# Attention rows: where denominators and numerators stand on the tensor engine, and which PSUM banks they use

## The chip, the core and the metric

The kernel runs on one core of one Trainium2 chip. The core's engines work side by side and each takes its own instructions strictly in order: the tensor engine (PE) multiplies matrices into PSUM, the vector engine (DVE) and the scalar engine (ACT) read PSUM and SBUF and write back, GpSimd (POOL) does little here, and the sync engine (SP) issues most of the DMAs. An instruction starts when its engine has come to it and the semaphores it waits for are set. PSUM has eight banks of 128 partitions by 512 float32 values. The metric is the device time of one execution in microseconds (us); lower is better.

## The reference

Two blocks of gated cross-attention and feed-forward work on `x` (8 batches of 512 tokens, 512 wide). The change lies in the first attention, which is linear attention with 16 heads of 32:

```
q    = feature_map(layernorm(x) @ Wq.T)          # x+1 if x>0 else exp(x)
gate = sigmoid(layernorm(x) @ Wg.T + bg)
k, v = split(ctx @ Wkv.T);  k = feature_map(k)
kv_summary = einsum('bhsd,bhse->bhde', k, v);  k_sum = k.sum(axis=-2)
z    = 1.0 / (einsum('bhld,bhd->bhl', q, k_sum)[..., None] + EPS)
attn = einsum('bhld,bhde->bhle', q, kv_summary) * z
x    = x + tanh(g_xattn[0]) * (attn * gate) @ Wo.T
```

The denominators are the einsum under `z`, the numerators the one with `kv_summary`. Everything after it (a feed-forward block, a softmax attention, an expert block) is untouched. All arithmetic is float32.

## The kernel before

**Rows.** The attention stage is a loop over the eight batches; the text calls a batch a row, 0 to 7. Each of the three large products of a row (Q, G for the gate, and O for the output) is done in seven block products instead of eight, in the order 1, 2, 6, 5, 7, 4, 3. One block product is four matmuls of 128x128 by 128x256 in the program, eight records in the profile, since each float32 matmul makes two passes. Products 1, 6, 7, 4 accumulate in a bank called x, 5 and 3 in w, and 2 in z, so that the rows of the profile say `x_q`, `w_g`, `z_xa_down` and so on (`xa_down` is O).

**Order by hand.** `steps` gives the first five products of a unit and keeps 4 and 3 back until the next unit's first product is done. In row b the program therefore lists Q1, O4, O3 (of row b-1's output), Q2, Q6, Q5, Q7; then G1, Q4, Q3, G2, G6, G5, G7; then O1 (the output of row b-1), G4, G3, O2, O6, O5, O7. The output of a row is one row late, because its attention needs the row's denominators spread out over the partitions.

**Order by a scheduler.** In this stage `in_order` holds neither the tensor nor the vector nor the scalar engine. What the program lists for these three is put in its final order, engine by engine, by a scheduler when the kernel is built; at run time the order is fixed. While `"tensor"` is in `in_order`, PE keeps the listed order: that is done around the numerators.

**The parts that the steps speak of.**

- `features` (L613 to L621): two ACT activations, relu and exp (L619, L620), then one DVE operation that writes a part of `q` (L621). After Q3 the last part takes a DVE addition (`qs_q`, L1157), the two activations and L621.
- `denominators` (L1187): four 32-column matmuls of `q` with `ksum` into one bank `pd`; DVE adds epsilon into `z` (L1195); two reciprocals of 128x256 (L1198); `z` goes to DRAM (`over`), and `spread` reads it back broadcast over the partitions. It is a generator, and each `next` lists one more of these pieces. Before, its first piece (matmuls and L1195) is listed at O1.
- `gated` (L1212) multiplies the gate's `th` by what `spread` brought, in the next row's Q.
- `numerators` (L1219): sixteen 32x32 matmuls of `q` with `summary` into four banks `pn0` to `pn3`.
- `attended` (L1232): DVE multiplies each `pn` by `th` into `a` (L1243, four operations of 128x512), and forms the sums s1, s2 and a difference (`combine_inner`, L895 to L897). O1 reads `a`.
- `GUp` (L1164): the gate. It writes `th`, a tile that has **one buffer** (pool `attention_units`, `bufs=1`), with additions on DVE (L1178) and tanh on ACT (L1183); the additions free the banks z, w of G.
- `normed` (L471): the norm of row b+1, with four ACT operations `xn_xa` and four transposes `pt_xa` on PE into PSUM, copied by ACT (L517).

**PSUM.** Pool `ps` has four banks, shared in turn by `pt_xa`, `pd` and `pn`. Pool `acc` has four, used in turn by the x, w and z banks of Q, G and O. `numerators` takes all four `ps` banks at once.

**Listing before.** In row b, the numerators of row b-1 and `attended` are listed between Q7 and G1; the denominators of row b at O1:

```
        if done:
            attended(done[0], done[2], numerators(*done[0:2]))
        g = GUp(b)
        den = denominators(b, q.q)
```

Row 0 has no earlier row: all of its denominators' pieces are listed after G7. Row 7 has nothing after it: the pieces of its denominators are listed from G6 on, and its numerators follow G7 in the same row.

Of the kernel before, what the change touches and what calls it, by code (L numbers as in the profile page):

```python
# [21 lines left out]
F32 = mybir.dt.float32  # L22
# [6 lines left out]
PSUM = bass.MemoryType.PSUM  # L29

P = 128
B, S, D = 8, 512, 512
# [11 lines left out]
H2 = 256  # L44
# [24 lines left out]
def flamingo_kernel(  # L69
# [40 lines left out]
    phase = ExitStack()  # L110
# [5 lines left out]
    bank = {"ps": ps}  # L116

    def psum(name):
        return bank["ps"].tile([P, 512], F32, tag="ps", name=name)

    idle_banks = []

    def acc_bank(name):

        if not idle_banks:
            return bank["acc"].tile([P, 2, H2], F32, tag="acc", name=name), None
        assert len(idle_banks) > 0
        n = idle_banks.pop(0)
        return bank["acc"].tile([P, 2, H2], F32, tag=f"acc{n}", name=name, bufs=1), n

    def temp(name):
        return work.tile([P, 512], F32, tag="t2", name=name, bufs=8)

    def halves(t):

        return t.rearrange("p (n t) -> p n t", t=H2)
# [25 lines left out]
    def load_x(ph, b):  # L162
        if ph == "xa0" and b % 4 == 3:
            t = awork.tile([P, NT, D], F32, tag="x4", name=f"x_{ph}{b}")
        else:
            t = work.tile([P, NT, D], F32, tag="x", name=f"x_{ph}{b}", bufs=3)
        if ph == "xa0":
            src = x[ts(b, S), :].rearrange("(t p) d -> p t d", p=P)
        else:
            src = between[ph, b]  # L170

        queue = nc.scalar if ph == "xa0" and b > 1 else nc.sync
        with here("scalar"):
            queue.dma_start(out=t, in_=src)
        xs[ph, b] = t
# [3 lines left out]
    def flush():  # L179
        while stores:  # L180
            store_x(*stores.pop(0))
# [468 lines left out]
    def cross_attention(b):  # L650
# [63 lines left out]
        yield  # L714

        lent, n = acc_bank(f"pr_{b}_3")
        idle_banks.append(n)
        pr = [psum(f"pr_{b}_{t}") for t in range(3)] + [lent.rearrange("p n t -> p (n t)")]
# [91 lines left out]
    OPENS, CLOSES = (1, 5, 2), (4, 3, 2)  # L810

    class Unit:
# [5 lines left out]
        def step(self, m):  # L818
            name = BANK[m]
            if m in OPENS:  # L820
                self.banks[name], self.numbers[name] = acc_bank(f"{name}_{self.tag}")
            self.product(m, self.banks[name])
            self.after(m, self.banks[name])
            if m in CLOSES and self.numbers[name] is not None:
                idle_banks.append(self.numbers[name])

        def weights(self, m):
# [64 lines left out]
    def combine_inner(at, prefix=""):  # L892

        a11, a12, a21, a22, s1, s2 = (inner[prefix + k][:, at, :] for k in INNER)
        nc.vector.tensor_tensor(s1, a21, a22, ALU.add)  # L895
        nc.vector.tensor_tensor(s2, s1, a11, ALU.subtract)
        nc.vector.tensor_tensor(a21, a11, a21, ALU.subtract)  # L897
# [97 lines left out]
    class SplitDown(Unit):  # L995
# [6 lines left out]
        OPENS, CLOSES = (2, 4, 1, 5), (2, 4, 7, 3)  # L1002
# [70 lines left out]
        def gated(self, dst, src):  # L1073
            nc.vector.scalar_tensor_tensor(dst, src, GATE[self.ph], dst, ALU.mult, ALU.add)
# [111 lines left out]

    def denominators(b, q):  # L1187

        pd = psum(f"pd_{b}")
        for c in range(NC):  # L1190
            nc.tensor.matmul(pd[ts(c, HD), :], lhsT=kv[b][1][:, c, :], rhs=q[:, c, :], start=True, stop=True)
            in_order.add("tensor")
        in_order.discard("tensor")
        z = temp(f"z_{b}")
        nc.vector.tensor_scalar(z, pd, ATT_EPS, None, ALU.add)  # L1195
        yield
        for r in range(2):
            nc.vector.reciprocal(z[:, ts(r, H2)], z[:, ts(r, H2)])  # L1198
            yield
        over[b] = dram.tile([P, S], F32, tag=f"over{b}", name=f"over_{b}")  # L1200
        nc.sync.dma_start(out=over[b], in_=z)
        yield
# [16 lines left out]
    def numerators(b, q):  # L1219

        summary = kv[b][0]
        pn = [psum(f"pn{h}_{b}") for h in range(NC)]
        in_order.add("tensor")
        for c in range(NC):
            for h in range(NC):
                rows = ts(h, HD)
                nc.tensor.matmul(
                    pn[h][ts(c, HD), :], lhsT=summary[rows, c, :], rhs=q[rows, c, :], start=True, stop=True
                )
        return pn  # L1230

    def attended(b, th, pn, ahead=lambda b, th, half: None):  # L1232

        if b < B - 1:
            a = aunits.tile([P, 2, 2, 2, H2], F32, tag="a", name=f"a_{b}")
        else:
            a = work.tile([P, NC, S], F32, tag="xnT", name=f"a_{b}").rearrange(
                "p (r c) (n t) -> p r c n t", c=2, n=2
            )
        for h in range(NC):  # L1240
            if h % 2 == 0:
                ahead(b, th, h // 2)
            nc.vector.tensor_tensor(  # L1243
                a[:, :, h // 2, h % 2, :], halves(th[:, h, :]), halves(pn[h]), ALU.mult
            )
        for k in ("s1", "s2"):
            inner["x" + k] = aunits.tile([P, 2, H2], F32, tag=k, name=f"{k}_xa0_{b}")
        for r in range(2):
            for c in range(2):
                inner[f"xa{r + 1}{c + 1}"] = a[:, r, c]  # L1250
        combine_inner(slice(0, 2), "x")
# [12 lines left out]
    def steps(units, late=late):  # L1264

        for u in units:
            for n, m in enumerate(u.order[: u.head]):
                yield u, m
                if n == 0:
                    yield from late  # L1270
                    late.clear()
            late.extend((u, k) for k in u.order[u.head :])
# [9 lines left out]
    def some(prep):  # L1282
        if prep not in ready and next(prep, None) == "last":
            ready.add(prep)
# [50 lines left out]
        pass  # L1335
    set_aside()
    first.close()
    bank["acc"] = phase.enter_context(tc.tile_pool(name="acc", bufs=4, space=PSUM, reuse_waits="tile"))
    aunits = phase.enter_context(tc.tile_pool(name="attention_units", bufs=1, reuse_waits="tile"))
    in_order -= {"tensor", "vector", "scalar"}  # L1340
    builder = build_first()
    done = None
    ticks = iter(range(10**6))

    def tick():

        if next(ticks) % 2:
            next(builder, None)

    for b in range(B):  # L1350
        prep = work_list[b + 1][2]
        if b == B // 2 + 1:
            nc.vector.tensor_scalar(b2_sb, b2_sb, gate_ff0, None, ALU.mult)
        q = QUp(b)
        for n, (u, m) in enumerate(steps([q])):
            u.step(m)
            if done and n in (1, 3):
                gated(done[0], done[2], n // 2)
            if b == B - 1 and n == 1:
                load_x("ff0", 0)  # L1360
            if n == 4:
                flush()
                if b < B - 1:
                    some(prep)
            tick()
        if done:
            attended(done[0], done[2], numerators(*done[0:2]))
        g = GUp(b)
        den = denominators(b, q.q)
        for n, (u, m) in enumerate(steps([g])):  # L1370
            u.step(m)
            in_order.discard("tensor")
            tick()
            if n == 1:
                if b + 2 < B:
                    load_x("xa0", b + 2)
                elif b + 1 == B:
                    load_x("ff0", 1)
            if b == B - 1 and n > 3:
                next(den, None)  # L1380
            if n == 3 or n > 3 and not done:
                some(prep)
        if not done:
            for _ in den:
                pass
            spread(b)
        if b == B - 1:
            for _ in den:
                pass
            spread(b)  # L1390
            pn = numerators(b, q.q)
        for n, (u, m) in enumerate(steps([ODown(done[0])] if done else [])):
            u.step(m)
            in_order.discard("tensor")
            if b < B - 1:
                next(den, None)
                if n == 6:
                    spread(b)
            elif n == 6:
                attended(b, g.th, pn, gated)  # L1400
            if n in ((0, 1, 3, 5) if b < B - 1 else (6,)):
                some(prep)
            tick()
        for _ in prep:
            pass
        done = b, q.q, g.th
# [52 lines left out]
    for u, m in [*steps([ODown(B - 1)]), *late]:  # L1459
# [6 lines left out]
        ps=stack(tc.tile_pool(name="ff_ps", bufs=3, space=PSUM, reuse_waits="tile")),  # L1466
        acc=stack(tc.tile_pool(name="ff_acc", bufs=1, space=PSUM, reuse_waits="tile")),
    )
    idle_banks += range(5)
    bank["ringb"] = stack(tc.tile_pool(name="ringb", bufs=1, reuse_waits="tile"))  # L1470
    for _ in range(MORE):
        next(loads)
# [125 lines left out]
```

## Time and profile before

| | us |
|---|---|
| median of three runs | 2057.13 (2056.67 to 2058.53) |
| the profiled execution, its own time | 2056.86 |
| its span in the profile | 2055.1 |
| PE busy | 2040.4 |
| DVE busy | 1501.5 |
| ACT busy | 629.3 |
| attention stage of rows 1 to 7, first numerators to the first feed-forward product | 81.25 to 378.07 |

The page says that a busy PE is not PE at its peak. A matmul is pipelined: one pass of 128x256 is recorded with some 0.38 us, but eight of them that follow each other start every 1.73 us together. The views that the prediction uses are the timelines of the engines (start, duration, engine, line, operation, tiles, count, and in brackets the idle time before with the instruction that ended it), the table by stretches of time, and the list of waits.

The critical chain on the page is of the end of the execution and does not reach back to the attention stage, so the stage has to be read from the timelines.

### The profile page before, as it was taken

How to read it: one execution, taken by the hardware profiler on the slowest of the kernel's cores; microseconds unless marked ns; L12 is line 12 of the kernel's file. 1: busy time of each engine (PE TensorE's matmuls, PEld its weight loads, DVE VectorE, ACT ScalarE, POOL GpSimd, SP SyncE). 2: the span in 40 equal slices, each digit the busy share in tenths (PEclk: the TensorE clock that was granted, in tenths of full speed). 3: DMA queues.
4: the chain of work that ended last, by engine and by line, in shares of the span. 5: the costliest groups of instructions: out<-in, count | busy, mean ns of one | idle time of the engine just before them, and what ended most of it. 6: DMA issues, size and time to landing. Idle time of an engine off the chain costs nothing. (4 is left out here: it accounts for less than half of the span.)

```text
span 2055.1 us, 35088 instructions
## 1 busy us (share of the span) xinstructions
PE 2040.4 (99%) x12796; PEld 1814.5 (88%) x12796; DVE 1501.5 (73%) x2989; ACT 629.3 (31%) x1294; POOL 97.7 (5%) x124
## 2 busy tenths in 40 slices
PE   9999999999999999999999999999999999999998
PEld 5888887898989999999989898898989898898988
DVE  4787888575758677676859676877777776777758
ACT  4533443323242423233242322213122222212121
POOL 3000000000000000000001010100000010100000
PEclk9999999999999999999999999999999999999999
DMA  6376546698888887888868768585867768585865
GB/s 203 132 220 193 180 140 192 237 299 278 300 280 280 280 295 249 293 278 282 294 218 284 228 195 281 172 283 178 281 201 242 231 197 279 174 282 155 275 204 170
DMA packets 304235, 484.67 MB, mean 236 GB/s; under 512 B 37056, under 2 KB 103776, under 8 KB 299968
## 3 DMA queue, kind: packets, MB, share of 16 engines
q1 hardware_dynamic: 296624, 455.65, 69.6%
q10 hardware_dynamic: 5856, 23.20, 3.1%
q0 software_dynamic: 1584, 3.57, 0.7%
q8 instruction: 103, 1.69, 0.3%
q14 instruction: 68, 0.56, 0.1%
HBM read 413.04 MB, written 69.27 MB: 235 GB/s over the span
## 5 line engine op out<-in xcount | busy, mean ns | idle before, releaser
L856 PE MATMUL x_ff<-S_ff,w_ff 128*128 128x256 f32 x1280 | 304.2, 380 | 0.0
L856 PE MATMUL w_ff<-S_ff,w_ff 128*128 128x256 f32 x1280 | 303.4, 380 | 0.0
L856 PE MATMUL x_ff<-xnT_ff,w_ff 128*128 128x256 f32 x1280 | 294.5, 379 | 0.0
L868 ACT COPY u_ff<-x_ff 128x512 f32<-128x512 f32 x240 | 139.9, 584 | 475.4 <-PE x_ff L856 447.6
L856 PEld LDWEIGHTS x_ff<-S_ff,w_ff 128*128 128x128 f32 x1280 | 240.5, 190 | 40.2 <-issue 6.5
L856 PEld LDWEIGHTS w_ff<-S_ff,w_ff 128*128 128x128 f32 x1280 | 239.0, 190 | 32.2 <-issue 1.4
L856 PEld LDWEIGHTS x_ff<-xnT_ff,w_ff 128*128 128x128 f32 x1280 | 237.8, 190 | 30.8 <-ACT a_ff L916 0.4
L1051 PE MATMUL x_ff_down<-w_ff_down,split_ff_down 128*128 128x128 f32 x1344 | 157.9, 275 | 0.0
L1051 PEld LDWEIGHTS x_ff_down<-w_ff_down,split_ff_down 128*128 128x128 f32 x1344 | 153.9, 192 | 0.0
L856 PE MATMUL z_ff<-xnT_ff,w_ff 128*128 128x256 f32 x640 | 151.4, 379 | 0.0
L1065 DVE TENSOR_TENSOR part_ff_down<-part_ff_down 128x128 f32<-128x128 f32 x315 | 85.3, 288 | 67.5 <-ACT part_ff_down L1078 60.1
L856 PEld LDWEIGHTS z_ff<-xnT_ff,w_ff 128*128 128x128 f32 x640 | 119.8, 190 | 15.3
L1051 PE MATMUL w_ff_down<-w_ff_down,split_ff_down 128*128 128x128 f32 x896 | 105.3, 275 | 0.0
L1051 PEld LDWEIGHTS w_ff_down<-w_ff_down,split_ff_down 128*128 128x128 f32 x896 | 102.6, 192 | 0.0
L911 DVE TENSOR_TENSOR a_ff<-w_ff,u_ff 128x512 f32<-128x512 f32 x64 | 43.9, 686 | 72.8 <-ACT u_ff L868 72.7
L916 ACT ACTIVATE a_ff<-a_ff,b_sb 128x256 f32<-128x256 f32 x128 | 58.1, 501 | 94.1 <-DVE a_ff L911 94.1
L939 DVE SCALAR_TENSOR_TENSOR g_ff<-th_ff,x_ff 128x512 f32<-128x512 f32 x48 | 32.8, 684 | 70.3 <-ACT th_ff L938 70.3
L1051 PE MATMUL w_ff_down<-w_ff_down,s_ff 128*128 128x128 f32 x672 | 81.5, 275 | 0.0
L1051 PE MATMUL x_ff_down<-w_ff_down,a_ff 128*128 128x128 f32 x672 | 80.4, 275 | 0.0
L1051 PEld LDWEIGHTS w_ff_down<-w_ff_down,s_ff 128*128 128x128 f32 x672 | 79.4, 192 | 0.8
L1051 PEld LDWEIGHTS x_ff_down<-w_ff_down,a_ff 128*128 128x128 f32 x672 | 78.4, 192 | 0.5
L949 DVE TENSOR_TENSOR up_ff<-w_ff,u_ff 128x512 f32<-128x512 f32 x96 | 65.6, 684 | 17.7 <-ACT u_ff L868 17.7
(258 smaller groups left out, 3328.3 us busy)
## 6 DMA issues: line engine op xcount, KB each, us to landing
w_ff_down<-stream_ff SPq DMA_DIRECT2D x680, 256.0 KB
w_ff<-ff_up SPq DMA_DIRECT2D x560, 256.0 KB
stream_ff<-build_ff_down SPq DMA_DIRECT2D x49, 448.0 KB
x_ff<-x_ff SPq DMA_DIRECT2D x16, 1024.0 KB
share<-shares SPq DMA_DIRECT2D x64, 256.0 KB
ff_up<-build_ff_up SPq DMA_DIRECT2D x42, 256.0 KB
x_ff<-x_xa ACTq DMA_DIRECT2D x8, 1024.0 KB
x_ff<-x_ff ACTq DMA_DIRECT2D x8, 1024.0 KB
```

The costliest lines, as they stand in the source:

```text
L856: nc.tensor.matmul(p[:, n, :], lhsT=w[:, c, ts(n, P)], rhs=moving, **self.mark(m, 2 * n + c),)
L868: nc.scalar.copy(self.s[m], p)
L911: nc.vector.tensor_tensor(h, p, s, ALU.add)
L916: nc.scalar.activation(h[:, n, :], p[:, n, :], AF.Gelu, bias=b1_sb[:, f : f + 1])
L939: nc.vector.scalar_tensor_tensor(g, th, 1.0, p, ALU.add, ALU.mult)
L949: nc.vector.tensor_tensor(u, p, s, ALU.add)
L1051: nc.tensor.matmul(p[bank][:, place, :], lhsT=operand[k][:, c, :], rhs=w[at // 4][:, ts(at % 4, P)], start=bank not in opened, stop=True, ...
L1065: return lambda: nc.vector.tensor_tensor(m(k), m(k), m(by), ALU.add)
```

## The change

Three things are edited.

1. **The place.** The numerators of row b-1 with `attended` are no longer listed before G1. They are listed at step 5 of G, after G5, and directly ahead of them `next(den, None)` lists the denominators' matmuls and the addition that makes `z`. The next pieces move up by one step: in rows 1 to 6 the two reciprocals and the DMA are listed at O1, G4 and G3 (before: at G4, G3 and O2). In row 7 they are listed from G7 on, and in row 0 after G7.
2. **The bank.** `pd` no longer comes from pool `ps`. It takes a bank out of the list `idle_banks` and puts it straight back at the end of the list, so it is lent by the accumulators.
3. **The accumulators' banks.** Pool `acc` has four named banks with one buffer each. `acc_bank` takes the one that has been idle longest, and a unit gives its bank back when its last product on it is done. The fall-back to a rotating pool is gone.

```diff
     def acc_bank(name):
-        if not idle_banks:
-            return bank["acc"].tile([P, 2, H2], F32, tag="acc", name=name), None
-        assert len(idle_banks) > 0
         n = idle_banks.pop(0)
         return bank["acc"].tile([P, 2, H2], F32, tag=f"acc{n}", name=name, bufs=1), n
...
-            if m in CLOSES and self.numbers[name] is not None:
+            if m in CLOSES:
                 idle_banks.append(self.numbers[name])
...
     def denominators(b, q):
-        pd = psum(f"pd_{b}")
+        pd, n = acc_bank(f"pd_{b}")
+        idle_banks.append(n)
+        pd = pd.rearrange("p n t -> p (n t)")
...
-    bank["acc"] = phase.enter_context(tc.tile_pool(name="acc", bufs=4, space=PSUM, reuse_waits="tile"))
+    bank["acc"] = phase.enter_context(tc.tile_pool(name="acc", bufs=1, space=PSUM, reuse_waits="tile"))
+    idle_banks += range(4)
...
-        if done:
-            attended(done[0], done[2], numerators(*done[0:2]))
         g = GUp(b)
         den = denominators(b, q.q)
         for n, (u, m) in enumerate(steps([g])):
             u.step(m)
             in_order.discard("tensor")
+            if n == 5:
+                next(den, None)
+                if done:
+                    attended(done[0], done[2], numerators(*done[0:2]))
             tick()
...
-            if b == B - 1 and n > 3:
+            if b == B - 1 and n > 5:
                 next(den, None)
...
-    idle_banks += range(5)
+    idle_banks[:] = range(5)
```

## The prediction, made before the changed kernel had run

> **What bounds the kernel now.** First the page's busy shares: PE is busy for almost the whole span and at full granted clock throughout, so a microsecond of PE idleness in any stage is a microsecond of time.
>
> ```profile
> PE 2040.4 (99%) x12796; PEld 1814.5 (88%) x12796; DVE 1501.5 (73%) x2989; ACT 629.3 (31%) x1294; POOL 97.7 (5%) x124
> PEclk9999999999999999999999999999999999999999
> ```
>
> Then the table by stretches, cut at the first numerator record of rows 1 to 7 (stretch; length, busy time and count by engine):
>
> ```profile
> 81.25:121.67 40.42, 40.42 (x225) 33.70 (x224) 33.04 (x56) 17.04 (x31) 1.21 (x2) 1.00 0.56 165
> 121.67:163.72 42.05, 40.97 (x225) 33.55 (x225) 32.56 (x53) 17.13 (x31) 4.39 (x2) 1.00 0.81 243
> 163.72:204.98 41.26, 40.96 (x225) 33.54 (x224) 36.43 (x57) 16.89 (x31) 2.18 (x2) 1.00 0.57 174
> 204.98:245.41 40.43, 40.43 (x225) 33.71 (x224) 32.48 (x54) 17.43 (x31) 1.70 (x2) 1.00 0.53 174
> 285.84:326.94 41.10, 40.70 (x225) 33.63 (x224) 33.49 (x54) 17.42 (x31) 1.58 (x2) 1.00 0.55 180
> ```
>
> A clean row lasts 40.42; three rows are longer, by 1.63, 0.84 and 0.68: 3.1 us of stalls in rows 2, 3 and 6. The list of PE's waits between 60 and 380 us agrees: `x_g` behind ACT's `u_g` copy, `x_xa_down` behind DVE, and in row 7 `pd` twice behind L621 (0.7 and 0.4). So the stage has little to win: 3.1 us of stalls, about 2 us in row 7, and changes of tile size on PE. It has much to lose, because PE has no slack and DVE is 80% busy.
>
> What the change can save on PE stands in the timeline of row 5 (start, duration):
>
> ```profile
> 203.16 1.89 PE L856 MATMUL x_q<-S_xa,w_q 128*128 128x256 f32 x8
> 204.98 1.14 PE L60 MATMUL pn<-q,summary 32*32 32x512 f32 x32
> 206.05 1.99 PE L60 MATMUL x_g<-xnT_xa,w_g 128*128 128x256 f32 x8
> 207.88 1.89 PE L856 MATMUL x_q<-xnT_xa,w_q 128*128 128x256 f32 x8
> 209.61 1.89 PE L856 MATMUL w_q<-S_xa,w_q 128*128 128x256 f32 x8
> ```
>
> Read the differences of starts: a product takes 1.73 (207.88 to 209.61), 1.82 when `pn` follows and 1.83 behind it. Numerators cost 1.07 plus 0.09 and 0.10 for changing the tile size. The denominators in the same way: 1.82 before them, 1.00 (220.06 to 221.06), 0.05 behind.
>
> **Part 1: the two follow each other.** The Trainium skill, "TensorEngine Tiling (Array Packing)", Key Properties, says that changing the tiling mode drains the engine and changing only the tile does not. By that rule 128x32 after 32x32 is still a change, so four changes a row become three, not two. By the row: 0.09+0.05+0.09+0.10 = 0.33 becomes 0.09+0.05+0.10 = 0.24. Saved: 0.1 us a row; by a reading in which "follow each other" means one mode, 0.15. I take 0.1 in each of rows 1 to 6: **-0.6** (row 7 below).
>
> **Part 2: DVE's order.** In the built program of the changed kernel DVE's order in every row 1 to 7 is: last `q` (L621), `z` (L1195), both reciprocals, and only then the four products `a`, then `th` from `z_g`. Before, the `a` ran 9 to 12 us ahead of `z` (209.04 to 212.91 in row 5). Now they queue behind it:
>
> ```profile
> 221.20 0.69 DVE L1195 TENSOR_SCALAR z<-pd 128x512 f32<-128x512 f32 x1 [0.27 <-PE pd L60]
> 221.92 3.37 DVE L1198 RECIPROCAL z<-z 128x256 f32<-128x256 f32 x2
> ```
>
> `z` starts 0.14 after PE has gone on from `pd` (221.06); the reciprocals end at 225.29. Call E the moment PE leaves `pd`: reciprocals end at E+4.2, the first `a` (0.68) at E+4.9, the next three 0.60 apart (E+5.5, 6.1, 6.7).
>
> On PE, after E: `pn` 1.07, G7 with its change of size 1.83, so at E+2.9 it comes to the first transpose `pt_xa` of the next row's norm. Its PSUM bank is the one of `pn0` (four `ps` banks, all four taken by `pn`), and in the built program it waits for the first `a`. It is at the head of PE's queue; G4, O1 and all else stand behind it. Stall: 4.9-2.9 = **2.0 us a row**, rows 1 to 6: **+12.0**. In before this transpose stood about 16 us behind `pn`.
>
> Here a rule decides. "VectorE: DVE Perf Modes", Walkthrough, Mode 1x, in the Trainium skill gives one result a cycle; with 0.96 GHz ("Trainium Kernel Development and Optimization", NeuronCore Architecture) a 256-wide reciprocal would be an estimated 0.27 us, the first `a` would be done at E+2.1, and there would be no stall. The row says 1.69 each (3.37 for two), six times that; the same page remarks that a reciprocal is an iterative divide with a repeat count of 8, by which it would be an estimated 2.1 each and the stall 2.9. I take the row.
>
> **Part 3: q comes late for pd.** `pd` moves from 5 products after Q3's end (G2, G6, G5, G7, O1) to 3. Let T be the start of G2 (211.34 in row 5); `pd` is due at T+5.27. Its third matmul needs the last L621. ACT's built order in rows 1 to 5 is relu, the copy `u_g` of G6, exp; the copy waits for G6:
>
> ```profile
> 214.99 0.59 ACT L868 COPY u_g<-x_g 128x512 f32<-128x512 f32 x1
> 215.47 0.63 ACT L620 ACTIVATE fe_q<-fe_q 128x512 f32<-128x512 f32 x1
> ```
>
> exp ends at 216.10 = T+4.76, L621 (0.68, no longer behind the `a`) at T+5.5, `pd` goes on at 5.55: 0.3 late. If the two halves of `pd` do not overlap, it is up to 1.0 (row 7 of before shows two halves of 0.98 each). Below nothing is excluded: PE is at the instruction already. I take 0.3, five rows: **+1.5** (0 to 5). In row 6 exp is ahead of the copy: 0.
>
> **Part 4: th has one buffer.** `th` of row b may be written only when the `a` of row b-1 have read it, so G's additions stand behind the four `a`: `z_g` is freed at E+7.3 (a's end 6.7, plus 0.6). By disuse, O1 gets just that bank and waits for it. PE, after the stall: transpose 0.5, G4 1.73, so at O1 at E+7.15: +0.15 in rows 1, 2, 4, 5, 6. In row 3 a 128x896 operation of the weight building (1.08, L60) stands between: +1.1. G3 then waits for the `th` of `w_g` (E+9.1) about when PE gets there: 0.3 in all. The other transposes wait for ACT's `xn_xa`, which stand behind `th`'s tanh: I find them at about E+10.8 when PE needs them at E+10.85; nothing, but without margin. Sum **+2.2** (0 to 4). `pd`'s own lent bank was `w_q`'s, long read: nothing.
>
> **Part 5: what goes.** The 3.1 us in rows 2, 3 and 6 came of L621, `qs_q` and `u_g` behind the `a`, sums and building work on DVE. With the `a` moved behind `pd`, the q chain has DVE to itself: **-3.1** (0 if other work takes the place).
>
> **Part 6: rows 0 and 7, the tail.** Row 7: both numerators stand on either side of G7. The second set needs all four banks of the first, so it finishes about 1.0 behind the last `a`: E+7.7 = T+14.0 with E = T+6.3 (exp is early here). Before, from T (333.30) to its end (344.97) it was 11.67, without the first set (1.17). So 14.0-1.2-11.7 = **+1.1**, in which the two stalls of `pd` that go (1.1) and its halves (1.0) are already counted. Row 0: `pd` is cut by a transpose after its first matmul, which costs one more half, 1.0, and fills 0.4 that PE filled with other work anyway: **+0.6**. Tail to 378: `z` of row 7 is ready 3.7 earlier against T, so the 0.57 stall at 369.35 (DVE) may go: **-0.5**.
>
> SP's queue has the same DMAs in the same order; `over` is issued earlier after its row's `pd` and nothing is moved past it. POOL is as before in this stage. From the first feed-forward product on, the orders of PE, DVE and ACT are the same in both kernels, and the list of waits has 0.8 us for PE there in all, so nothing gives the loss back.
>
> **Sum.** -0.6+12.0+1.5+2.2-3.1+1.1+0.6-0.5 = +13.2 us. On the profiled execution's own time of 2056.86 (1.8 around its span of 2055.1) that is 2070.1; on the median 2057.13 it is 2070.3. I say **2070**.
>
> **Rivals.**
>
> *A. The stall is there and nothing else is won* (the old stalls stay in other places, `pd` in two halves): parts 3 at 5 and 5 at 0 give 13.2+3.5+3.1 = +19.8, 2077. For it: DVE's load a row is the same 33 us, only moved. Against: the q chain is what stalled PE, and it is now ahead of everything.
>
> *B. Faster: the stall is not there.* One mechanism: the first `a` is done before PE reaches the transpose, at E+2.9. Place: DVE between `z` and `a`. It needs the two reciprocals to last 1.4 together or less instead of 3.37. Then part 2, part 4 and about 2 us of row 7's wait fall away (12.0+2.2+2.0): 13.2-16.2 = -3.0, 2054. Against: 16 reciprocals of before, median 1.74.
>
> *C. The stall is hidden*: other waits of PE in the rows already hold the same time, so that only the change in rows 0 and 7 shows: 2057 to 2060. Against: four of the six rows had none.
>
> *D. The change doesn't do what it says:* excluded by the built order for rows 1 to 7 (`pd`, then `pn`, with nothing between); it fails only in row 0, where there is nothing above.
>
> **Numbers.** The forecast's own case 0.82, A 0.12, C 0.04, B 0.02. Range: low, parts 3 and 4 at nothing and rows 0 and 7 at half: 13.2-4.5=+8.7, 2065.5, less a little for a shorter stall, 2064; high, to most of A, 2076. Under 0.2% (4.1 us), about what a measurement of this kernel can't tell from no change: slower 0.95, same 0.04, faster 0.01.
>
> **What would show it.** In the profile after, the first `pt_xa` of each of rows 1 to 6 with about 2.0 us of idle PE before it, released by DVE `a` L1243; reciprocals directly ahead of the `a`; rows of about 42.8 between numerators; the waits for `u_g` and `qs_q` gone; `pd` with about 0.3 of idle or two halves; `pn` of row 7 waiting 2 us and more for `a`. Wrong: rows of 40 us, or the `a` ahead of the reciprocals in time, or idle PE of another kind that outweighs this one.

## The result, and the profile after

| | before | after |
|---|---|---|
| median (lowest to highest), six runs each | 2057.63 (2056.67 to 2059.22) | 2073.49 (2072.39 to 2074.59) |
| profiled execution, its own time / span | 2056.86 / 2055.1 | 2072.94 / 2071.2 |
| first feed-forward product starts at | 378.07 | 394.16 |
| from there to the end of the span | 1677.0 | 1677.0 |

The ratio is 1.0077, 95% interval [1.0067, 1.0087]: slower by 15.9 us; 2070 was forecast, 2064 to 2076 the range. All of it (394.16-378.07 = 16.09) arises in the attention stage, none comes back later. Line numbers after are one to three lower than before (L1194 is `z`, L1197 the reciprocals, L1242 `a`, L511 the transposes, L618 the last part of `q`).

The busy row of the page, and the table by stretches cut at the first numerator of rows 1 to 7 (stretch; length; busy time and count of PE, weight loads, DVE, ACT, POOL; granted clock; DMA):

```profile
PE 2045.7 (99%) x12796; PEld 1816.0 (88%) x12796; DVE 1503.1 (73%) x2989; ACT 629.8 (30%) x1294; POOL 97.0 (5%) x124
```

```profile
93.69:137.48 43.79, 41.85 (x226) 33.67 (x224) 33.74 (x53) 17.00 (x31) 2.59 (x2) 1.00 0.61 173
137.48:180.45 42.97, 41.07 (x226) 33.67 (x224) 32.94 (x54) 17.22 (x31) 1.71 (x2) 1.00 0.58 175
180.45:223.14 42.69, 40.86 (x226) 33.75 (x224) 33.88 (x53) 17.34 (x31) 1.70 (x2) 1.00 0.66 196
223.14:266.12 42.98, 41.09 (x227) 33.68 (x225) 32.42 (x52) 17.23 (x31) 1.58 (x2) 1.00 0.52 164
308.80:352.38 43.58, 41.15 (x228) 33.48 (x224) 38.40 (x64) 17.82 (x32) 1.59 (x2) 1.00 0.56 167
```

A row lasts 42.7 to 43.8 where it lasted 40.4 to 42.1, and the second column (PE busy) has grown far less than the length: PE stands still for the rest. PE's list of waits between 55 and 400 us names the reason (who waits, for whom; sum, times, longest):

```profile
PE pt_xa L511 <- DVE a L1242: 10.9, 6, 1.8
PE pn L60 <- DVE a L1242: 1.7, 1, 1.7
PE x_q L853 <- ACT u_q L865: 0.6, 1, 0.6
PE x_xa_down L969 <- DVE x_xa L985: 0.5, 1, 0.5
```

One row of it, row 4, in the timelines of PE and of DVE (start, duration, instruction, idle time before with its releaser):

```profile
223.14 1.14 PE L60 MATMUL pn<-q,summary 32*32 32x512 f32 x32
224.21 1.99 PE L60 MATMUL x_g<-S_xa,w_g 128*128 128x256 f32 x8
228.04 0.63 PE L511 MATMUL pt_xa<-ident,xn_xa 128*128 128x128 f32 x4 [1.83 <-DVE a L1242]
230.46 1.99 PE L969 MATMUL x_xa_down<-w_o,a 128*128 128x256 f32 x8
232.29 1.97 PE L853 MATMUL w_g<-S_xa,w_g 128*128 128x256 f32 x8
```

```profile
223.26 0.69 DVE L1194 TENSOR_SCALAR z<-pd 128x512 f32<-128x512 f32 x1 [1.15 <-PE pd L60]
223.99 3.37 DVE L1197 RECIPROCAL z<-z 128x256 f32<-128x256 f32 x2
227.27 2.41 DVE L1242 TENSOR_TENSOR a<-th,pn 128x512 f32<-128x512 f32 x4
```

PE leaves `pd` at 223.14 (the moment that the prediction calls E) and could go on from `pn` and G7 at 226.04 (224.21 and 1.83 behind). It then waits until 228.04, E+4.90, for the first `a`, which DVE takes up at 227.27, when both reciprocals are through. The lateness is 2.00; the 1.83 in brackets is shorter only because the record of G7 runs on a little. Before, the first transpose of this row stood behind `pd` and waited for nothing:

```profile
221.06 0.66 PE L514 MATMUL pt_xa<-ident,xn_xa 128*128 128x128 f32 x4
```

(The row that the prediction calls row 5 is row 4 when the first is 0; no number hangs on it.)

### The profile page after: what moved, and what is told of

It is laid out like the page before. It is cut to its first block, busy times and chain, and to the rows that moved or that the text cites. A ratio compares the mean times of both kernels' runs of the same rounds, so it can differ in the third digit from the quotient of the medians.

```text
span 2071.2 us, 35115 instructions
## 1 busy us (share of the span) xinstructions
PE 2045.7 (99%) x12796; PEld 1816.0 (88%) x12796; DVE 1503.1 (73%) x2989; ACT 629.8 (30%) x1294; POOL 97.0 (5%) x124
## 4 chain that ended last, share of the span: by engine, by line
PE 94%; DVE 4%; issue 0%; ACT 0%; DMA 0%; POOL 0%; SPq 0%; ACTq 0%; DVEq 0%; POOLq 0%
PE x_ff L853 27%; PE w_ff L853 13%; PE x_ff_down L1048 13%; PE w_ff_down L1048 8%; PE z_ff L853 7%; PE z_ff_down L1048 4%; PE v_ff_down L1048 4%; PE x_xa_down L969 2%; PE x_q L853 2%; PE x_g L853 1%; PE pt_ff L511 1%; PE pt_xa L511 1%; PE w_g L853 1%; PE w_xa_down L969 1%; DVE z L1197 1%; PE w_q L853 1%
```

## The experiments

Edits are shown against the changed kernel, `...` marks lines left out. The theory: the stall needs two things together, reciprocals ahead of `a` on DVE and a transpose that needs `pn0`'s bank soon behind `pd` on PE. Rivals: the banks do it; each of the two moves costs by itself; `pd` comes too early for `q`. Before is at 2056.8 to 2057.7 beside the experiments, the changed kernel at 2073.5.

### The banks alone

The lent bank and the four named accumulators, with the listing of before.

```diff
+        if done:
+            attended(done[0], done[2], numerators(*done[0:2]))
         g = GUp(b)
...
-            if n == 5:
-                next(den, None)
-                if done:
-                    attended(done[0], done[2], numerators(*done[0:2]))
...
-            if b == B - 1 and n > 5:
+            if b == B - 1 and n > 3:
```

> The kernel before with the change's banks alone: pd in a bank lent by the accumulators, accumulators by disuse; numerators and denominators stand where they stood. Theory: no cost, 2057.6 within 1 us. Rival 2 (the going round by disuse gives O1 or others a bank that is read late): new waits of PE on th or z, 2060 or more.

Measured: 2057.79, ratio 1.0002 [0.9994, 1.0010]. In the old places the banks cost and bring nothing.

### The place alone

The new listing, with the banks of before.

```diff
...
-        pd, n = acc_bank(f"pd_{b}")
-        idle_banks.append(n)
-        pd = pd.rearrange("p n t -> p (n t)")
+        pd = psum(f"pd_{b}")
...
-    bank["acc"] = phase.enter_context(tc.tile_pool(name="acc", bufs=1, space=PSUM, reuse_waits="tile"))
-    idle_banks += range(4)
+    bank["acc"] = phase.enter_context(tc.tile_pool(name="acc", bufs=4, space=PSUM, reuse_waits="tile"))
```

> Denominators and numerators in their new place, but with the banks of before: the denominators take a bank of the ps ring and the accumulators a ring of four. Theory: pn3 then gets the bank of pd and waits for z, about 0.8 after PE leaves pd, but the first transpose still waits for the first a at the same moment after that (pn0's bank), so the wait in front of the transpose shrinks by as much: the same time as the changed kernel, 2073.5 (2071 to 2076). Rival (the lent bank is worth something in this place): 0.8 in each of rows 1 to 6 on top, 2078.

Measured: 2069.22, ratio 1.0052 [1.0037, 1.0068], below both expectations. PE's timeline of the same row:

```profile
221.99 2.00 PE L60 MATMUL pn<-q,summary 32*32 32x512 f32 x32
223.92 1.99 PE L60 MATMUL x_g<-S_xa,w_g 128*128 128x256 f32 x8
226.80 1.99 PE L971 MATMUL x_xa_down<-w_o,a 128*128 128x256 f32 x8 [0.89 <-DVE a L1242]
228.63 0.60 PE L513 MATMUL pt_xa<-ident,xn_xa 128*128 128x128 f32 x4
229.07 1.89 PE L855 MATMUL x_g<-xnT_xa,w_g 128*128 128x256 f32 x8
```

The numerators do wait for `z` (1.93 from start to start instead of 1.07), and the next thing still comes at `a` (E+4.81). But the scheduler has put O1 ahead of the transpose here, and O1 waits for `a`: O1, transpose and G4 end at E+8.81 instead of E+9.15 (232.29-223.14). Six times 0.34 and the 0.8 by which row 0 is shorter make 2.8, about the 2.6 by which the two profiled executions differ (2072.94 and 2070.32). In the new place the change's banks thus cost 2.6 by the profiles and 4.3 by the medians, through the order that the scheduler chose with them, and about three quarters of the loss is the place.

### a ahead of the reciprocals

DVE keeps the listed order of `a` and reciprocals (`here` fixes it), and the same in rows 1 to 6 or row 7 alone.

```diff
+            with here(*(["vector"] if b > 0 else [])):
-            nc.vector.reciprocal(z[:, ts(r, H2)], z[:, ts(r, H2)])
+                nc.vector.reciprocal(z[:, ts(r, H2)], z[:, ts(r, H2)])
...
+            with here(*(["vector"] if b < B - 1 else [])):
-            nc.vector.tensor_tensor(
+                nc.vector.tensor_tensor(
...
```

> The changed kernel with one thing different: on DVE the four products a are held ahead of both reciprocals in rows 1 to 7. Theory (reciprocals ahead of the first a hold PE at the first transpose): the first a is done at E+1.6 instead of E+4.9, so the six stalls of 2.0 us go (-12), the second numerators of row 7 wait at most 0.5 (-3), and with them the half clock that the profile shows there (-1.7): about 2073.5-17 = 2056.5, within 2 us of before. Rival 1 (the late numerators, th with one buffer or the lent banks cost the time, and the reciprocals only fill it): PE waits elsewhere for about as long, 2068 or more.

> The changed kernel with the a held ahead of the reciprocals in row 7 alone (numerators of row 6). It tells what row 7 adds. Theory, with the half clock caused by the broken-up work of PE there: -3.2 for the wait and -1.7 for the clock, 2068.6, with a granted clock of 1.00 in that stretch. If the clock falls for another reason: -3.2 alone, 2070.3, and the clock low as before. Rows 1 to 6 keep their stalls of 2.0.

> The changed kernel with the four products a ahead of the two reciprocals on DVE in rows 1 to 6 only; row 7 is listed as in the changed kernel. Before is at 2057.6, the changed kernel at 2073.5, the same order in rows 1 to 7 at 2065.2. Theory (the wait of the transpose for a is the price of rows 1 to 6, and the loss that was left with the order in all rows sits in row 7 and the tail, where reciprocals put behind a make the scale of row 7 late): rows 0 to 6 cost 1.6 over before as in that run, row 7 and the tail 2.0 as in the changed kernel, together 2061.2 (2060 to 2063), and the 2.7 us wait of z_xa_down in the tail is gone. Rival (what was left is spread over the rows, the price of q coming late and of the one th buffer): 2065, as with all seven rows.

| `a` ahead in | median | ratio and interval | rows 1 to 6, first `pn` of row 1 to that of row 7 | from there to the feed-forward |
|---|---|---|---|---|
| none (changed kernel) | 2073.49 | 1.0077 [1.0067, 1.0087] | 258.69 | 41.78 |
| rows 1 to 7 | 2065.18 | 1.0042 [1.0029, 1.0056] | 246.91 | 44.74 |
| row 7 | 2073.39 | 1.0078 [1.0063, 1.0093] | 258.83 | 42.27 |
| rows 1 to 6 | 2061.45 | 1.0019 [1.0012, 1.0026] | 246.91 | 40.98 |

In rows 1 to 6 the order is worth 11.8 (258.69-246.91), and the wait of the transpose is gone. That this is so near the 12.0 of the sum is in part luck, for 11.8 is a balance: the stalls (11.9), the waits of O1 and G3 behind them (2.1) and the wait of `x_q` (0.8) go, but `q` now comes later against PE at `pd`, which takes 1.26 to 3.04 where it takes 1.00 when nothing is late; that lateness grows from 2.1 to 5.0 in the six rows. PE's timeline of row 4 with `a` ahead in rows 1 to 7:

```profile
217.57 1.14 PE L60 MATMUL pn<-q,summary 32*32 32x512 f32 x32
218.64 1.99 PE L60 MATMUL x_g<-S_xa,w_g 128*128 128x256 f32 x8
220.47 0.60 PE L511 MATMUL pt_xa<-ident,xn_xa 128*128 128x128 f32 x4
```

The first two runs missed on row 7, where the expectations had a gain of 4.7 to 4.9. With row 7 alone, the gain comes where it was looked for: from G2 to G4 of row 7 PE needs 12.98 instead of 17.43, the second numerators do not wait, and the clock stays at 1.00 there. But 4.94 are lost again in the tail. The reciprocals of row 7 end 5.3 later, the DMA of `z` is issued at 361.99 instead of 356.64, and the last operations that multiply row 7's `th` by the scale come at 377.75 instead of 372.12 and 374.77, its last `a` behind them. Just before, DVE stands 1.5 for ACT, so part of the lateness is the order of the tail; the shares were not separated. PE and DVE with row 7 alone:

```profile
379.69 3.23 PE L969 MATMUL z_xa_down<-w_o,a 128*128 128x256 f32 x8 [2.43 <-DVE a L1244]
```

```profile
377.75 1.28 DVE L1215 SCALAR_TENSOR_TENSOR th<-th,spread 128x512 f32<-128x512 f32 x2
378.96 1.27 DVE L1244 TENSOR_TENSOR a<-th,pn 128x512 f32<-128x512 f32 x2
```

With rows 1 to 6 alone that wait is absent and the time is 0.25 beside the one expected: the theory stands. 3.8 us over before are left. In rows 1 to 6 that is the late `q` (5.0), less the old stalls (3.1) and the saved changes of tile size (0.7); the rest lies in row 0, row 7 and the tail and was not taken apart.

### Two reciprocals more

Rows 1 to 7 get two reciprocals more ahead of `a` (the value is turned over twice more); `here` holds `a` behind all four.

```diff
         nc.vector.tensor_scalar(z, pd, ATT_EPS, None, ALU.add)
+        if b:
+            with here("vector"):
+                for r in range(2):
+                    nc.vector.reciprocal(z[:, ts(r, H2)], z[:, ts(r, H2)])
+                for _ in range(2):
+                    nc.vector.reciprocal(z[:, 0:H2], z[:, 0:H2])
         yield
         for r in range(2):
-            nc.vector.reciprocal(z[:, ts(r, H2)], z[:, ts(r, H2)])
+            if not b:
+                nc.vector.reciprocal(z[:, ts(r, H2)], z[:, ts(r, H2)])
...
```

> The changed kernel with two more reciprocals of 128x256 in each row 1 to 7 (the first half of z is inverted three times, which leaves its value), all four ahead of the a on DVE. Theory: the first a comes 3.37 us later in seven rows, PE has nothing else to do, so +3.4 in each: +23.5, 2097. If a longer idle of PE also brings the half clock seen in row 7, about 1.5 more in each row, 2107. Rival 1 (the reciprocals only fill time that PE waits anyway): less than +8, 2081 or less.

Measured: 2101.45, ratio 1.0212 [1.0196, 1.0227], 28.0 over the changed kernel, between the two numbers of the theory (+23.5 and +33.5). The rival is refuted. PE's timeline of row 2, where PE leaves `pd` at 141.21:

```profile
142.28 1.99 PE L60 MATMUL x_g<-S_xa,w_g 128*128 128x256 f32 x8
144.95 1.99 PE L853 MATMUL x_g<-xnT_xa,w_g 128*128 128x256 f32 x8 [0.68 <-ACT u_g L865]
149.42 0.66 PE L511 MATMUL pt_xa<-ident,xn_xa 128*128 128x128 f32 x4 [2.47 <-DVE a L60]
```

The transpose comes at E+8.21 instead of E+4.90: 3.31 later for 3.37 of reciprocals. So the wait follows what DVE does ahead of `a`. The time does so only by balance: here the scheduler has put G4 ahead of the transpose, which fills 1.7 us of each wait, and the clock is halved behind the stall in all seven rows (below). In row 4, for instance, 3.3 later, 2.1 saved with G4 and the waits behind it, and 1.8 lost by the half clock and a short wait of O2 make 3.0.

### One move at a time, and both one product later

Numerators alone late (denominators at O1 as before); denominators alone early (numerators ahead of G as before); the latter, and the changed kernel, one product of G later. The new place, behind G5 in the listing, is called "behind G6" in the expectations.

```diff
             if n == 5:
-                next(den, None)
                 if done:
                     attended(done[0], done[2], numerators(*done[0:2]))
...
-            if b == B - 1 and n > 5:
+            if b == B - 1 and n > 3:
```

```diff
+        if done:
+            attended(done[0], done[2], numerators(*done[0:2]))
         g = GUp(b)
...
             if n == 5:
                 next(den, None)
-                if done:
-                    attended(done[0], done[2], numerators(*done[0:2]))
```

```diff
-            if n == 5:
+            if n == 6:
```

> Only the numerators move to their new place behind G6; the denominators stay where they were before (rows 1 to 6 behind O1), with the change's banks. Theory (the stall needs both: reciprocals ahead of a on DVE, and the transposes ahead of a's end on PE): here a runs ahead of the reciprocals, O1 stands between G7 and the first transpose, and the q chain has DVE to itself, so the stalls of before in rows 2, 3 and 6 (3.1) may go: 2055.5 (2054.5 to 2058). Rival (each of the two moves costs by itself, the numerators through the one th buffer, which keeps z_g's bank taken until a has read th): at least a third of the 16 us, 2063 or more.

> Only the denominators move to their new place behind G6; the numerators of the row above stay ahead of G as before, with the change's banks. Theory (the stall needs both): a is long done when the reciprocals come, so no transpose waits; but PE is at pd three products behind Q3 and the last q is behind a, sums and building work on DVE, so pd waits 0.3 to 1.0 in each of rows 1 to 6 and goes in two halves: +1.8 to +6, 2060.5 (2059 to 2064). Rival (early reciprocals cost by themselves, whatever a does): half the 16 us or more, 2066.

> As the denominators moved alone (2066.3), but one product of G later: PE reaches pd 1.73 us later, after four products since Q3 instead of three. Theory (its 8.7 us are PE standing at pd before q is there: the second half of pd started 7.3 to 8.3 after the start of G2 in rows 1 to 4, where PE was due at 5.3): PE is then due at 7.0, so the wait shrinks to 0.1 to 1.0 a row, 2060 (2058.5 to 2061.5). Rival (z and the reciprocals ahead of other work on DVE cost by themselves, wherever q stands): 2065 or more.

> The changed kernel with both, denominators and numerators, one product of G later. Before 2057.7, changed 2073.5. Theory (the price is that a stands behind pd, z and two reciprocals on DVE while PE needs a about 3 after pd, and that distance moves along; only q's lateness of 0.3 a row and the halves of pd in row 2, together 2, go away): 2071.5 (2069.5 to 2073). Rival (the price is that pd comes too early for q, as where the denominators move alone): the loss falls with it to 2065 or less.

| | median | ratio and interval |
|---|---|---|
| numerators alone | 2057.34 | 0.9997 [0.9989, 1.0006] |
| denominators alone | 2066.33 | 1.0042 [1.0027, 1.0057] |
| denominators alone, one product later | 2063.70 | 1.0031 [1.0020, 1.0042] |
| both, one product later | 2081.33 | 1.0113 [1.0096, 1.0129] |

**Numerators alone** cost nothing: O1 stands between G7 and the transpose, and `a` runs ahead of `z`. PE's timeline of row 4:

```profile
213.52 1.14 PE L60 MATMUL pn<-q,summary 32*32 32x512 f32 x32
214.59 1.99 PE L60 MATMUL x_g<-S_xa,w_g 128*128 128x256 f32 x8
216.42 1.89 PE L969 MATMUL x_xa_down<-w_o,a 128*128 128x256 f32 x8
218.15 0.27 PE L511 MATMUL pt_xa<-ident,xn_xa 128*128 128x128 f32 x1
```

No wait of PE is recorded in rows 1 to 6, so the 3.1 us of stalls of before are gone. From Q2 of row 1 to Q2 of row 7 that gives 2.2 (243.68 instead of 245.86; the rest went to more switching of tile sizes: one transpose, `pd`, three transposes), but the feed-forward starts only 0.5 earlier (377.55), since row 7 and the tail take 1.6 more, where `pn` waits 0.8 for `a`.

**Denominators alone** cost 8.7, which is the number of the rival, not of the theory, but not by the rival's mechanism. Row 2, PE and then DVE:

```profile
135.22 0.62 PE L1190 MATMUL pd<-q,ksum 128*32 128x512 f32 x1 [0.50 <-DVE qs_q L1154]
137.62 1.91 PE L60 MATMUL pd<-q,ksum 128*32 128x512 f32 x4 [1.35 <-DVE q L618]
```

```profile
130.89 2.47 DVE L1242 TENSOR_TENSOR a<-th,pn 128x512 f32<-128x512 f32 x4
133.28 0.68 DVE L618 SCALAR_TENSOR_TENSOR q<-qs_q,fe_q 128x512 f32<-128x512 f32 x1
133.88 0.68 DVE L892 TENSOR_TENSOR s_xa<-a 128x512 f32<-128x512 f32 x1
134.48 0.68 DVE L1154 TENSOR_TENSOR qs_q<-w_q,u_q 128x512 f32<-128x512 f32 x1
135.68 0.68 DVE L894 TENSOR_TENSOR a<-a 128x512 f32<-128x512 f32 x1
136.89 0.68 DVE L618 SCALAR_TENSOR_TENSOR q<-qs_q,fe_q 128x512 f32<-128x512 f32 x1
```

The last part of `q` stands behind `a` and its sums, and PE is at `pd` first: PE's list has 4.8 us of `pd` behind `q` in four places and none behind a reciprocal. (The first wait, 0.50, is not for an input: `qs_q` reads the bank `w_q`, which `pd` borrows. The prediction had put this at nothing; it happens in this one row.) The later version agrees that it is `q`: no `pd` waits, and from row 1's numerators to row 7's it takes 248.66 us instead of 254.46 (before: 245.69). What is left over before is mostly `x_g`, which waits 4.2 in all, in five places, for ACT's copy `u_g`; in row 2 this copy stands on ACT behind an activation that waits for `qs_q`, so there it is the lateness of `q` again. The median of the later version, 2063.70, lies between the theory's number and the rival's. From row 7's numerators to the feed-forward it takes 55.0 where before takes 51.1: there `x_xa_down` waits 3.8 for DVE's `x_xa`, and the clock is halved once.

**Both, one product later** missed both expectations. The wait in front of the transpose is there as the theory has it, recorded with 2.2 instead of 1.8 in each of the six rows; `pd` does not wait, but in rows 2 and 3 it goes in two halves. And another price joins. PE's timeline of row 4:

```profile
232.58 0.69 PE L511 MATMUL pt_xa<-ident,xn_xa 128*128 128x128 f32 x4 [2.18 <-DVE a L1242]
233.08 1.05 PE L853 MATMUL x_g<-xnT_xa,w_g 128*128 128x256 f32 x2
233.93 3.17 PE L969 MATMUL z_xa_down<-w_o,a 128*128 128x256 f32 x8
```

Behind the stall TensorE is granted half its clock, and eight records that take 1.89 take 3.17. The table by stretches of 3.41 us (third number: PE busy; last three columns: granted clock, DMA share, GB/s) shows the stall of row 4, the stretch behind it, and the stalls of rows 2 and 3, behind which the clock stays at 1.00:

```profile
229.66:233.07 3.41, 1.23 (x8) 0.81 (x7) 3.41 (x5) 0.00 (x0) 0.00 (x0) 1.00 0.00 0
233.07:236.49 3.42, 3.42 (x10) 2.53 (x9) 3.39 (x7) 2.43 (x6) 0.00 (x0) 0.50 0.00 1
140.91:144.32 3.41, 1.75 (x22) 1.06 (x6) 3.41 (x3) 0.00 (x0) 0.00 (x0) 1.00 0.48 153
185.28:188.70 3.42, 1.59 (x20) 1.06 (x6) 3.42 (x3) 0.00 (x0) 0.00 (x0) 1.00 0.57 163
```

The last section says why these stretches were taken.

### Numerators late in rows 1 to 6 only

```diff
+        if done and b == B - 1:
+            attended(done[0], done[2], numerators(*done[0:2]))
         g = GUp(b)
...
-                next(den, None)
-                if done:
+                if done and b < B - 1:
...
-            if b == B - 1 and n > 5:
+            if b == B - 1 and n > 3:
```

> The numerators move behind G6 only in rows 1 to 6 (those of rows 0 to 5); in row 7 they stay ahead of G as before, and the denominators stay where they were in every row, with the change's banks. Before is at 2057.7, the numerators moved in all rows 2057.3. Theory (that move gains about 2.2 in rows 1 to 6, where the stalls in front of x_g and x_xa_down go, and gives 1.7 of it back in row 7, where the second set of numerators waits for the four a of the first): 2055.5 (2054.5 to 2057.0), no wait of pn for a in row 7. Rival (what row 7 gave back comes from rows 1 to 6 having only shifted their waits onto row 7): 2057.5, as with all rows.

Measured: 2059.63, ratio 1.0009 [1.0003, 1.0016], worse than both. Rows up to row 7's first `pn` are 1.6 ahead of before (325.34 against 326.94), but the feed-forward starts at 379.90, 1.8 behind it: in row 7 and the tail `x_xa_down` waits 3.4 us for DVE's `x_xa`. What the scheduler makes of the tail differs from version to version, and no version found is faster than before beyond doubt.

## Why the prediction was right, and where it was off

The differences of the profiled executions, by `z_g` starts and the start of the feed-forward (in rows 1 and 7 the numerators' 1.26 stand on different sides of `z_g` before and after; this is set right):

| | forecast | measured |
|---|---|---|
| row 0 | +0.6 | +0.8 |
| rows 1 to 6 | +12.0 | +13.25 |
| row 7 and the tail | +0.6 | +2.0 |
| sum | +13.2 | +16.1 |

The prediction was right in its mechanism, and 12 of the 16 us are its main term. The 2.9 us that are missing in the sum have three places: `pd` in row 2 (0.6), a wait of `x_q` that no term had (0.8), and row 7 with the tail (1.4).

- **Part 1, right.** The change from `pd` to `pn` shows at most 0.01 (in row 6 `pd` takes 1.00 and `pn` 1.08 from start to start), so 0.11 a row are saved, 0.7 against 0.6.
- **Part 2, right in mechanism and size.** The transpose comes at E+4.90, the lateness is 2.0 in rows 1 to 5 and 1.9 in row 6, 11.9 against 12.0. With `a` ahead this wait is gone, with two reciprocals more it moves by their length. The row of the trace was right for the reciprocals (3.37 for two) and the estimate of one result a cycle (0.27 each) would have forecast no stall. Rival B is refuted by the same row, C by the rows that had no stall before and are longer now.
- **Part 3, under-sized in one row.** `pd` takes 1.26 in rows 1, 3, 4 and 5 (0.26 late; forecast 0.3), 1.00 in rows 6 and 7, but 2.08 in row 2: there a `q` addition stood behind two pieces of weight building on DVE, and `pd` fell in halves. 2.1 instead of 1.5. Alone, without `a` moved out of `q`'s way, the early `pd` cost 8.7: the two moves help each other here, while through part 2 they hurt each other.
- **Part 4, right in its sum, by luck.** O1 waits 0.22 in rows 1, 2, 4 and 5 and 0.28 in row 6, but in row 3 it stands behind `z_xa_down` and the 1.1 does not come: 1.2 instead of 1.85. A cost that the term did not have stands in its place: behind a wait a product takes 1.83 to the next start instead of 1.73 (230.46 to 232.29), 0.5 in five rows. With 0.4 around G3 (forecast 0.3) that is 2.1 against 2.2.
- **Part 5, right, with a new wait beside it.** The old stalls went as forecast (3.1), but `x_q` in row 7's Q waits 0.57 by its record for ACT's copy, and costs 0.8 from start to start.
- **Rival A** (2077) is as near the measured time as the forecast is. Its mechanism did not come: the waits for `u_g` and `qs_q` are gone, and `pd` falls in halves in one row of six.
- **Part 6, the term that failed.** For row 7 and the tail +0.6 stood in the sum and +2.0 came. DVE was through with the last `a` on time (358.94, T+12.8), but the end of the second numerators, forecast for T+14.0, came at T+14.65, and the product behind them took 2.78 from start to start instead of 1.8. The clock was halved from 359.3 on, which no term had; with `a` ahead, where such numerators ran at a clock of 1.00, the product behind them took 1.83:

```profile
357.21 3.62 PE L60 MATMUL pn<-q,summary 32*32 32x512 f32 x32 [1.75 <-DVE a L1242]
360.76 2.94 PE L60 MATMUL x_xa_down<-w_o,a 128*128 128x256 f32 x8
```

```profile
359.00:360.00 1.00, 1.00 (x28) 0.22 (x26) 1.00 (x2) 0.30 (x1) 0.00 (x0) 0.65 0.16 59
360.00:361.00 1.00, 1.00 (x14) 0.24 (x2) 1.00 (x3) 0.71 (x3) 0.00 (x0) 0.50 0.50 176
361.00:362.00 1.00, 1.00 (x3) 0.82 (x4) 1.00 (x2) 0.81 (x2) 0.00 (x0) 0.50 0.60 180
```

The tail's stall of 0.5 stayed, but from G4 of row 7 on PE needs 30.62 instead of 31.27, with its transposes less broken up; so that -0.5 came about by luck, for another reason than the one given.

## What to carry to other kernels

When two pieces of work are listed side by side for the engine that is full, look at what they trigger on the next engine and in which order: here the moves alone cost 0 and 8.7, and 12 of the pair's 16 came of 3.4 us of reciprocals that got between the numerators and the only thing that frees their banks. A wait at the head of the full engine's queue holds all behind it; keep a product that is ready between a producer and the first taker of its banks, as O1 stood there with the numerators alone. The last iteration and the tail answer to their own deadlines, so a change that pays in the loop has to be costed there separately.

## What the runs showed of the hardware that was not expected

A stall can cost more than its length, by how it falls in time. In the changed kernel the six recorded idle times of 1.75 to 1.83 us in front of the transposes left the granted clock at 1.00. With both one product later the six were 2.17 to 2.18; behind four of them the clock fell to 0.50, behind the other two it stayed at 1.00. Two waits of the tail were equal as well, 2.28 in the later version of the denominators and 2.27 with the numerators late in rows 1 to 6: the first had a half clock behind it, the second had not.

The traces show a part of what decides. Read in stretches of 0.1 us, every drop lasts 3.41 us, two of them 6.83. Within one execution the drops begin at whole multiples of that time from each other: with both one product later at 99.95, 233.07, 277.45, 321.82 and 366.19, which are 39, 13, 13 and 13 times 3.413 us apart; with two reciprocals more the seven begin 14, 14, 13, 14, 13 and 15 times 3.413 us apart. So the drops keep to a grid of 3.41 us, and a stall seems to count by the share that it takes of one stretch of this grid. In the four rows with a drop PE was busy 0.36 of the stretch ahead of it; in the other two rows the emptiest stretch was busy 0.51 and 0.46. In the changed kernel, whose grid is known from its one drop, the emptiest stretch of each of the six stalls was busy 0.46 to 0.60.

The busy share alone does not sort all cases. With two reciprocals more, a stretch of 0.48 had a drop behind it and one of 0.42 had none. Stretches with many numerators or denominators had drops at 0.61 (row 7 of the changed kernel), 0.74 (the place alone) and 0.46 (row 2 with the denominators alone, 0.50 from 137.7 to 141.1). How much such small tiles count stays open.

The Trainium skill, "TensorE: Matmul & The Clock Gate", Part 1, has the clock halved after an idle window of about 3.4 us that runs freely. The length and the free running agree with these traces; a window of full idleness was not needed here, for PE was busy 0.21 to 0.74 of the stretch ahead of each drop.
